# Self attention's front: products by position set between dense products and emptied by three engines, and layer norms batch by batch with idle products

## The chip, the cores and the metric

The kernel runs on one core of a Trainium2 chip. The metric is the device time of one execution in microseconds (us), median of several runs. TensorE is written PE in the profile (PEld is its weight load), VectorE is DVE, ScalarE is ACT, GpSimd is POOL, SyncE is SP. A line such as L612 is line 612 of the kernel before.

## The reference, cut to what matters

One layer of a Perceiver: cross attention over a long context, self attention with relative positions, and a feed-forward that is itself an attention with gated heads. Each of the three begins with a layer norm over the 512 features, and each adds to x. B is 4, T is 128, D is 512, with 16 heads of 32. The part that the change touches is the self attention and the layer norms ahead of it and behind it:

```python
def _layernorm(x, axis=-1, eps=1e-05):
    m = jnp.mean(x, axis=axis, keepdims=True)
    v = jnp.var(x, axis=axis, keepdims=True)
    return (x - m) / jnp.sqrt(v + eps)
...
    q, k, v = (proj(Wq), proj(Wk), proj(Wv))
    a_q = Eq[rel]
    a_k = Ek[rel]
    a_v = Ev[rel]
    content = jnp.einsum('bhld,bhmd->bhlm', q, k)
    rel_k = jnp.einsum('bhld,lmd->bhlm', q, a_k)
    rel_q = jnp.einsum('bhmd,lmd->bhlm', k, a_q)
    pos_pos = jnp.einsum('lmd,lmd->lm', a_q, a_k)
    scale = 1.0 / hd ** 0.5
    logits = (content + rel_k + rel_q + pos_pos) * scale
    attn = jax.nn.softmax(logits, axis=-1)
    out = jnp.einsum('bhlm,bhmd->bhld', attn, v) + jnp.einsum('bhlm,lmd->bhld', attn, a_v)
...
x = x + xattn(_layernorm(x), ctx, ctx, ...)
x = x + attn(_layernorm(x), ...)
x = x + ffn(_layernorm(x), ...)
```

All is in float32. rel is the distance of two positions, cut to plus or minus 64.

## The kernel before

The kernel has three stages: cross attention (to about 650 us), self attention (to about 790 us) and the feed-forward. Inside a stage every engine works through its instructions in the order in which the program writes them (`manual_schedule`), and waits only where data or a buffer is not ready. So the order of the lines is the order of each engine's queue.

**The layer norm.** `layernorm_T` (L145) takes the rows of four batches from four banks of PSUM. For the second and third norm (L562 and L844) it takes its `else` branch. DVE computes statistics by batch (L157, L158), ACT the root of the variance plus eps (L161), DVE its reciprocal (L190, L198) and minus mean over deviation (`nmr`, L191). Batches are taken in two pairs: one root and one reciprocal serve two batches. The first pair is normalised on ACT (L169), the second on DVE (L165). Then each batch is turned on PE with four transposes (L214) into one of two banks, and that bank is copied to `xT`, by ACT for batches 0 and 1 and by DVE for 2 and 3 (L215). Last, ACT copies the four rows of x out of PSUM (L207).

**Projections.** `project_T` (L217) and `project` (L224) are four dense 128x512 products each; the trace has two instructions for each product. q is projected into the two pairs of banks of `banks("q")` (L649), in the order ps[2], ps[3], ps[0], ps[1], and drained with a scale (L652), by DVE for c even and ACT for c odd. k goes into three single banks and one more (`bank`, `bank_z`), drained at L657. `values(b)` projects v for one batch, drained by ACT (L646).

**Products by position.** `spread` (L593) copies q or k into `z`, laid out by position, in 16 copies (L598), of which 6 are on ACT and 10 on DVE. For each position there is then one product of a 32-row table slice with a 32x64 block of z. `by_position` (L605) does eight positions for each of four row groups: 32 products, 64 instructions of the trace, filling four banks. `relative_k(n)` (L623) does this for q into the two pairs of banks of `ps4`, and ACT copies the four banks to `rk` (L627). `relative_q(n)` (L629) does it for k into three single banks and `bank_z`, and DVE adds the table `pos` while it writes `lg` (L634).

**Logits.** `logits(c)` (L683) turns `rk` back with 16 transposes into the two pairs of `ps4` (L687) and adds 32 content products (L700). `join` (L713) adds `lg` on DVE (L716), `largest` finds the maxima (L722), and ACT takes exponentials (L727).

[...] In the self attention they are three for `bank`, one for `bank_z` and two pairs for `banks`. All of them were the cross attention's before. The first product of q waits for DVE's and ACT's last copies of the layer norm, the four copies of x (L207) among them; the later products of q don't wait for those again.

## Time and profile before

| what | value |
|---|---|
| median of 3 runs | 875.72 us (874.93 to 877.7) |
| the profiled execution's own time | 875.97 us |
| its span, first to last instruction | 874.1 us |
| mean granted TensorE clock | 0.980 |
| PE busy | 830.6 us (95%) |
| DVE busy | 628.2 us (72%) |
| ACT busy | 436.5 us (50%) |
| POOL busy | 430.6 us (49%) |

Busy time in stretches of 25 us around the change, in us, with the granted clock:

| stretch | PE | DVE | ACT | POOL | clock |
|---|---|---|---|---|---|
| 625 to 650 | 22.27 | 16.64 | 0.00 | 0.36 | 1.00 |
| 650 to 675 | 19.80 | 7.99 | 5.54 | 0.00 | 0.86 |
| 675 to 700 | 25.00 | 13.24 | 15.71 | 0.00 | 1.00 |
| 700 to 725 | 23.27 | 8.31 | 10.59 | 0.00 | 0.93 |
| 725 to 750 | 17.22 | 17.81 | 16.48 | 8.16 | 0.87 |
| 750 to 775 | 21.36 | 12.43 | 17.87 | 8.16 | 0.86 |
| 775 to 800 | 17.78 | 16.77 | 10.11 | 7.32 | 0.80 |

An engine counts as busy while an instruction of its own runs; register, branch and semaphore instructions and the issue of transfers don't count. Matmuls overlap in the pipeline, so a busy PE is not a PE at its best. The granted clock is the share of full speed at which TensorE was let run. Where an engine is idle, the profile names the instruction whose end released it.

### The profile page before, as it was taken

Reading aid. Unit: us, or ns where it says so; the run is one execution under the profiler, and the core shown is the slowest. Engines: PE = TensorE matmul, PEld = TensorE weight load, DVE = VectorE, ACT = ScalarE, POOL = GpSimd, SP = SyncE. Lnnn points to the kernel's source line nnn. Section 1 sums busy time; section 2 is a strip of 40 time slices with the busy share of each in tenths; the row PEclk is TensorE's granted clock in tenths of the full one; section 3 lists DMA queues with packets and bytes.
Section 4 is the critical chain, followed back from the end, with each engine's and each line's share of the span. In section 5 each row is a group of like instructions: output and inputs, shape, how many; then the busy total and the mean of one; then the engine's idle time right before and its main releaser. Section 6 shows DMA issues by size and latency. Waiting matters only on the chain. (4 is left out here: it accounts for less than half of the span.)

```text
span 874.1 us, 16373 instructions
## 1 busy us (share of the span) xinstructions
PE 830.6 (95%) x7061; PEld 447.9 (51%) x7061; DVE 628.2 (72%) x616; ACT 436.5 (50%) x721; POOL 430.6 (49%) x289
## 2 busy tenths in 40 slices
PE   9999999999999999999999999999898997779998
PEld 5454544554544545445445445544443466664564
DVE  2059788878888888888889888788861637556663
ACT  3357455564464554554554555644411736843671
POOL 1236666566656567575675665667500002512152
PEclk9999999999999999999999999999998998798999
DMA  8130010110101101010010101010100212001101
GB/s 300 50 124 2 1 49 1 49 49 1 50 1 49 49 2 49 1 49 13 37 49 1 49 1 49 1 36 15 49 28 21 96 50 98 1 2 51 49 1 49
DMA packets 10905, 35.53 MB, mean 41 GB/s; under 512 B 977, under 2 KB 1138, under 8 KB 8786
## 3 DMA queue, kind: packets, MB, share of 16 engines
q1 hardware_dynamic: 8402, 29.43, 9.7%
q10 hardware_dynamic: 1632, 3.15, 1.1%
q0 software_dynamic: 800, 1.93, 0.9%
q8 instruction: 55, 0.90, 0.4%
q14 instruction: 16, 0.13, 0.0%
HBM read 33.45 MB, written 1.05 MB: 39 GB/s over the span
## 5 line engine op out<-in xcount | busy, mean ns | idle before, releaser
L328 DVE TENSOR_TENSOR sg<-sg,stat 128x2048 f32<-128x2048 f32 x128 | 288.2, 2282 | 1.2
L337 ACT ACTIVATE sg<-sg 128x2048 f32<-128x2048 f32 x64 | 122.4, 1912 | 246.8 <-DVE sg L328 246.8
L227 PE MATMUL ps_v<-w_xattn_Wv,ct 128*128 128x512 f32 x512 | 231.5, 596 | 3.7 <-ACT v L274 3.7
L220 PE MATMUL ps_k<-ct,w_xattn_Wk 128*128 128x512 f32 x480 | 221.9, 605 | 0.8 <-ACT pos L142 0.8
L343 POOL TENSOR_TENSOR sm<-sm,sg 128x1024 f32<-128x1024 f32 x46 | 108.6, 2360 | 145.5 <-ACT sg L337 143.3
L307 DVE TENSOR_TENSOR mx<-mx,ps_s 128x1024 f32<-128x1024 f32 x96 | 117.2, 1221 | 78.1 <-ACT sg L298 65.9
L227 PEld LDWEIGHTS ps_v<-w_xattn_Wv,ct 128*128 128x128 f32 x512 | 95.8, 190 | 129.9 <-issue 113.5
L220 PEld LDWEIGHTS ps_k<-ct,w_xattn_Wk 128*128 128x128 f32 x480 | 86.2, 189 | 94.1 <-issue 86.1
L298 ACT COPY sg<-ps_s 128x1024 f32<-128x1024 f32 x128 | 124.2, 1020 | 7.2 <-DVE mx L305 3.5
L344 POOL TENSOR_TENSOR sm<-sm,sg 128x1024 f32<-128x1024 f32 x46 | 108.8, 2366 | 3.6
L275 POOL TENSOR_TENSOR v<-v,row_xattn_bv 128x512 f32<-128x512 f32 x64 | 81.6, 1276 | 40.0 <-ACT v L274 40.0
L734 POOL TENSOR_TENSOR lg<-lg,rs 128x512 f32<-128x512 f32 x16 | 16.3, 1041 | 120.9 <-issue 112.3
L285 PE MATMUL ps_s<-qT,kT 32*128 32x128 f32 x2048 | 75.7, 283 | 0.1
L372 PEld LDWEIGHTS pso<-sg,v 128*32 128x32 f32 x1920 | 48.8, 109 | 47.5 <-DVE mx L307 22.0
L285 PEld LDWEIGHTS ps_s<-qT,kT 32*128 32x128 f32 x2048 | 63.3, 186 | 18.0 <-issue 17.0
L372 PE MATMUL pso<-sg,v 128*32 128x128 f32 x1920 | 64.6, 276 | 3.7 <-DVE acc L385 2.1
L341 POOL TENSOR_TENSOR sm<-sg 128x1024 f32<-128x1024 f32 x16 | 37.9, 2366 | 45.3 <-ACT sg L337 45.2
L268 ACT ACTIVATE kT<-ps_k,bk 128x512 f32<-128x512 f32 x64 | 44.2, 694 | 10.4 <-PE ps_k L220 5.9
L274 ACT COPY v<-ps_v 128x512 f32<-128x512 f32 x64 | 36.4, 569 | 8.5 <-PE ps_v L227 8.4
L385 DVE TENSOR_TENSOR acc<-pso,acc 128x512 f32<-128x512 f32 x54 | 37.0, 684 | 3.9 <-PE pso L372 3.9
L305 DVE TENSOR_TENSOR mx<-sg,ps_s 128x1024 f32<-128x1024 f32 x16 | 19.5, 1220 | 27.3 <-ACT sg L298 27.3
L964 POOL TENSOR_TENSOR e<-e,rs 128x512 f32<-128x512 f32 x16 | 16.3, 1041 | 41.8 <-DVE rs L963 41.8
(208 smaller groups left out, 817.0 us busy)
## 6 DMA issues: line engine op xcount, KB each, us to landing
ct<-in_ctxT SPq DMA_DIRECT2D x15, 1024.0 KB, 4.9
ev_win<-in_tabv SPq DMA_DIRECT2D x1, 2048.0 KB, 7.1
w_xattn_Wk<-in_xattn_Wk ACTq DMA_DIRECT2D x4, 256.0 KB, 8.0
ct<-in_ctxT SPq DMA_DIRECT2D x4, 256.0 KB, 6.7
x<-in_x SPq DMA_DIRECT2D x4, 256.0 KB, 8.2
w_xattn_Wv<-in_xattn_Wv ACTq DMA_DIRECT2D x1, 1024.0 KB
w_xattn_Wq<-in_xattn_Wq SPq DMA_DIRECT2D x1, 1024.0 KB, 10.3
w_xattn_Wo<-in_xattn_Wo ACTq DMA_DIRECT2D x1, 1024.0 KB, 5.4
```

What stands on the lines that cost most here:

```text
L220: nc.tensor.matmul(ps, lhsT=w[:, k, c * P : (c + 1) * P], rhs=src[:, k, :], start=(k == 0), stop=(k == C - 1))
L227: nc.tensor.matmul(ps, lhsT=src[:, k, b * T : (b + 1) * T], rhs=w[:, k, :], start=(k == 0), stop=(k == C - 1))
L268: nc.scalar.activation(kT[n, c], ps, AF.Identity, bias=bk[:, c : c + 1])
L275: nc.gpsimd.tensor_tensor(v[n, b], v[n, b], bv_row, ALU.add)
L285: nc.tensor.matmul(ps[i][:, cols], lhsT=kT[n, c][rows, cols], rhs=qT[rows, c, cols], start=True, stop=True)
L298: nc.scalar.copy(sg[n, c][:, k * HALF : (k + 1) * HALF], pss[n, c][k])
L307: nc.vector.tensor_tensor(mxs[n], mxs[n], pss[n, c][k], ALU.max)
L328: nc.vector.tensor_tensor(g, g, stat[:, row, :].unsqueeze(1).to_broadcast([P, NH * B, T]), op)
L337: nc.scalar.activation(sg[n, c], sg[n, c], AF.Exp, scale=SCALE)
L343: eng.tensor_tensor(t, t, g[:, 0:HALF], ALU.add)
L344: eng.tensor_tensor(t, t, g[:, HALF:], ALU.add)
L372: nc.tensor.matmul(ps[i * HD : (i + 1) * HD, b * T : (b + 1) * T], lhsT=v[n, b][:, h * HD : (h + 1) * HD], rhs=sg[n, c][:, f * T : (f + 1) ...
```

## The change

In the layer norm's `else` branch the batches are no longer taken in pairs. Each batch has a root of its own right after its statistics. Batches 0 and 1 get their reciprocal, `nmr` and ACT normalisation after the root of the next batch; batches 2 and 3 are normalised on DVE after all statistics. The third turned batch is now copied by ACT, and only the fourth by DVE. A new function `idle` puts products of a zero tile (`warm`) with itself into a bank that nobody reads: six ahead of the first transposes, three between the second and the third, three behind the fourth. This holds for the norms at L562 and L844; the first norm of the kernel takes the other branch. `warm` is allocated earlier; the twelve products at the start of the kernel stay.

In the self attention, q is projected into the four single banks. The blocks by position are placed between projections: q0 to q3, k0 to k2, rk0, k3, rk1, v0, rk2, v1, rk3, half of v2, lg0, the other half, lg1, half of v3, lg2, the other half, lg3. The lg blocks now use the two pairs of `ps4`, as rk does. Their drains are split: banks 0 and 1 stay with DVE (with the addition of `pos`); banks 2 and 3 are copied by ACT and the addition is done in place by GpSimd, except in the last block, where DVE does all four. The spread of k is 3 copies on ACT and 13 on DVE; that of q is as before.

The diff:

```diff
--- before.py
+++ after.py
@@ -142,7 +142,13 @@
         nc.scalar.copy(pos, ps)
         yield
 
-    def layernorm_T(src, pool, n, before=None):
+    warm = const.tile([P, P], F32, tag="warm", name="warm")
+
+    def idle(ps, k):
+        for _ in range(k):
+            nc.tensor.matmul(ps, lhsT=warm, rhs=warm, start=True, stop=True)
+
+    def layernorm_T(src, pool, n, before=None, keep=None):
 
 
 
@@ -182,26 +188,37 @@
             for b in range(B):
                 turned(b)
         else:
-            first, second = slice(0, 2), slice(2, 4)
-            statistics(0)
-            statistics(1)
-            root(first)
-            statistics(2)
-            nc.vector.reciprocal(rstd[:, first], rstd[:, first])
-            nc.vector.scalar_tensor_tensor(
-                nmr[:, first], in0=mv[:, first, 0], scalar=-1.0, in1=rstd[:, first], op0=ALU.mult, op1=ALU.mult
-            )
-            normalised_act(0)
-            normalised_act(1)
-            statistics(3)
-            root(second)
-            nc.vector.reciprocal(rstd[:, second], rstd[:, second])
-            normalised(2)
-            normalised(3)
+            def inverse(b):
+                nc.vector.reciprocal(rstd[:, b : b + 1], rstd[:, b : b + 1])
+
+            def to_act(b):
+                inverse(b)
+                nc.vector.scalar_tensor_tensor(
+                    nmr[:, b : b + 1],
+                    in0=mv[:, b, 0:1],
+                    scalar=-1.0,
+                    in1=rstd[:, b : b + 1],
+                    op0=ALU.mult,
+                    op1=ALU.mult,
+                )
+                normalised_act(b)
+
+            for b in range(B):
+                statistics(b)
+                root(slice(b, b + 1))
+                if b == 1 or b == 2:
+                    to_act(b - 1)
+            for b in (2, 3):
+                inverse(b)
+                normalised(b)
+
+            keep(6)
             turned(0)
             turned(1)
-            turned(2, nc.vector.tensor_copy)
+            keep(3)
+            turned(2)
             turned(3, nc.vector.tensor_copy)
+            keep(3)
 
             for b in range(B):
                 nc.scalar.copy(x1[:, b, :], src[b])
@@ -385,11 +402,9 @@
                 nc.vector.tensor_tensor(acc[:, c, :], pso[n, c], acc[:, c, :], ALU.add)
 
 
-        warm = const.tile([P, P], F32, tag="warm", name="warm")
         nc.vector.memset(warm, 0.0)
         ps = ps_o.tile([P, B * T], F32, tag="pso", name="warm_ps")[:, 0:P]
-        for _ in range(12):
-            nc.tensor.matmul(ps, lhsT=warm, rhs=warm, start=True, stop=True)
+        idle(ps, 12)
 
         softplus()
         nc.scalar.activation(small.tile([P, 1], F32, tag="rt", name="rt0"), eps, AF.Sqrt)
@@ -559,7 +574,8 @@
         nc.scalar.activation(small.tile([P, 1], F32, tag="rt", name="rt"), eps, AF.Sqrt)
         project_out(3)
 
-        xT = layernorm_T(out_ps, ps_g, 1)
+        idle_ps = ps_o.tile([P, B * T], F32, tag="pso", name="idle_ps1")[:, 0:P]
+        xT = layernorm_T(out_ps, ps_g, 1, keep=lambda k: idle(idle_ps, k))
 
 
     awq = load_w("attn_Wq", nc.sync)
@@ -590,12 +606,12 @@
 
         z = big.tile([P, 2, NJ, NF], F32, tag="z", name="z")
 
-        def spread(src, n):
+        def spread(src, n, on_act):
             for g in range(NG4):
                 for i in range(NH):
                     from_ = src[i * HD : (i + 1) * HD].rearrange("p c (b g j) -> p g j c b", b=B, g=NG4)
                     to = z[g * HD : (g + 1) * HD, n].rearrange("p j (c i b) -> p i j c b", i=NH, b=B)
-                    (nc.scalar.copy if (g * NH + i) % 5 in (1, 3) else nc.vector.tensor_copy)(to[:, i], from_[:, g])
+                    (nc.scalar.copy if (g * NH + i) % 5 in on_act else nc.vector.tensor_copy)(to[:, i], from_[:, g])
 
 
         rk = big.tile([P, NF, T], F32, tag="rk", name="rk")
@@ -627,46 +643,60 @@
                 nc.scalar.copy(rk[:, :, positions(g, n)], ps[g].rearrange("p (j f) -> p f j", f=NF))
 
         def relative_q(n):
-            ps = [bank(f"lg{n}_{g}") for g in range(3)] + [bank_z(f"lg{n}_3")]
+
+
+            ps, _ = banks(f"lg{n}")
             by_position(tabq, 1, n * J8, ps)
             for g in range(NG4):
                 at = positions(g, n)
-                nc.vector.tensor_tensor(
-                    lg[:, :, at],
-                    ps[g].rearrange("p (j f) -> p f j", f=NF),
-                    pos[:, at].unsqueeze(1).to_broadcast([P, NF, J8]),
-                    ALU.add,
+                from_ = ps[g].rearrange("p (j f) -> p f j", f=NF)
+                pos_ = pos[:, at].unsqueeze(1).to_broadcast([P, NF, J8])
+                if g >= 2 and n + 1 < NJ // J8:
+                    nc.scalar.copy(lg[:, :, at], from_)
+                    nc.gpsimd.tensor_tensor(lg[:, :, at], lg[:, :, at], pos_, ALU.add)
+                else:
+                    nc.vector.tensor_tensor(lg[:, :, at], from_, pos_, ALU.add)
+
+        v = one.tile([P, B, D], F32, tag="v", name="v2")
+
+        def values(b, between=None):
+
+            ps = bank(f"v{b}")
+            for k in range(C):
+                if between and k == C // 2:
+                    between()
+                nc.tensor.matmul(
+                    ps, lhsT=xT[:, k, b * T : (b + 1) * T], rhs=awv[:, k, :], start=(k == 0), stop=(k == C - 1)
                 )
-
-        v = one.tile([P, B, D], F32, tag="v", name="v2")
-
-        def values(b):
-            ps = bank(f"v{b}")
-            project(ps, awv, xT, b)
             nc.scalar.copy(v[:, b, :], ps)
 
-
-        ps, _ = banks("q")
-        for c in range(C):
-            project_T(ps[c - 2], awq, xT, c)
-            (nc.scalar.mul if c % 2 else nc.vector.tensor_scalar_mul)(qT[:, c, :], ps[c - 2], SCALE)
-        spread(qT, 0)
-        for c in range(C):
+        def queries(c):
+            ps = bank(f"q{c}") if c < 3 else bank_z("q3")
+            project_T(ps, awq, xT, c)
+            (nc.scalar.mul if c % 2 else nc.vector.tensor_scalar_mul)(qT[:, c, :], ps, SCALE)
+
+        def keys(c):
             ps = bank(f"k{c}") if c < 3 else bank_z("k3")
             project_T(ps, awk, xT, c)
             (nc.scalar.copy if c % 2 else nc.vector.tensor_copy)(kT[:, c, :], ps)
-        spread(kT, 1)
+
+
+        for c in range(C):
+            queries(c)
+        spread(qT, 0, (1, 3))
+        for c in range(C - 1):
+            keys(c)
+        relative_k(0)
+        keys(C - 1)
+        relative_k(1)
+        spread(kT, 1, (1,))
         values(0)
+        relative_k(2)
         values(1)
-        relative_k(0)
-        relative_q(0)
-        values(2)
-        relative_k(1)
+        relative_k(3)
+        values(2, lambda: relative_q(0))
         relative_q(1)
-        values(3)
-        relative_k(2)
-        relative_q(2)
-        relative_k(3)
+        values(3, lambda: relative_q(2))
         relative_q(3)
         ev_win = big.tile([P, T, HD], F32, tag="z", name="ev_win")
         nc.sync.dma_start(
@@ -841,7 +871,8 @@
         for b in range(B):
             for c in range(C):
                 nc.tensor.transpose(out_ps[b][:, c * P : (c + 1) * P], oT[:, c, b, :], ident)
-        xT = layernorm_T(out_ps, ps1, 2)
+        idle_ps = bank_z("idle")[:, 0:P]
+        xT = layernorm_T(out_ps, ps1, 2, keep=lambda k: idle(idle_ps, k))
```

## The prediction

> **What bounds the kernel now.** I read the page first: TensorE is busy for 95% of a span of 874.1 us, so time is lost where it waits or runs at a low granted clock. The slices put both after 640 us. I then asked for busy time by stretches of a few microseconds from 640 us on, for the chain of waits there, and for the groups of instructions with their shapes. The chain from the layer norm to the first logits is TensorE almost throughout (start, length, what; us):

> ```profile
> 656.38 1.97 ACT x L207 x4
> 658.34 0.73 issue
> 659.08 5.82 PE s_q L220 x8
> ...
> 664.98 0.70 DVE qT L652
> ...
> 665.73 7.15 PE s_q L220 x16
> 672.90 0.70 DVE qT L652
> ...
> 673.64 3.70 PE s_q L220 x8
> 677.34 13.73 PE s_k L220 x32
> ...
> 701.71 0.69 DVE lg L634
> ...
> 702.44 3.70 PE s_v L227 x8
> ...
> 716.31 2.06 ACT rk L627 x4
> ...
> 721.33 2.82 PE s_lg L612 x48
> 724.15 3.60 PE s_l L687 x16
> ...
> 729.14 2.48 DVE lg L716 x4
> ```

> The reader is to see four losses, and that the first projection comes after ACT's copies of x. That projection (8 instructions) takes 5.82 us; 16 of them take 7.15 a little later. Twice a projection waits for DVE to empty the bank pair of the one before it (664.98, 672.90). The values wait for DVE in the same way (701.71, and again at 709.91). And from 721.33 to 729.14 products take about twice their time. The stretches say why (length, then busy us and instructions of PE, PEld, DVE, ACT, POOL, then granted clock):

> ```profile
> 653.10:656.50 3.40, 1.39 (x9) 0.95 (x10) 2.39 (x9) 2.82 (x6) 0.00 (x0) 1.00 0.81 283
> 656.00:660.00 4.00, 2.75 (x9) 1.84 (x10) 2.38 (x4) 2.33 (x5) 0.00 (x0) 0.57 0.18 71
> 714.70:718.10 3.40, 3.40 (x127) 3.40 (x120) 0.02 (x1) 2.05 (x5) 0.00 (x0) 1.00 0.63 205
> 718.10:721.50 3.40, 3.20 (x84) 2.80 (x85) 2.47 (x4) 1.49 (x4) 0.00 (x0) 0.99 0.29 108
> 724.00:728.00 4.00, 4.00 (x24) 3.59 (x24) 2.48 (x4) 0.00 (x0) 0.00 (x0) 0.50 0.68 262
> 728.20:731.61 3.41, 1.93 (x40) 1.57 (x33) 2.47 (x5) 0.00 (x0) 0.00 (x0) 1.00 0.65 269
> 789.70:793.10 3.40, 3.40 (x16) 2.64 (x14) 2.38 (x4) 2.78 (x7) 2.64 (x7) 0.50 0.84 214
> ```

> After 1.39 us of work in 3.4 (41%) the clock is halved, and after 84 products by position in 3.4 us as well; 127 of them kept it. Asked in stretches of 0.2 us, it falls at 656.5, 721.5, 745.3, 755.5 and 782.9 and returns at 663.3, 728.3, 748.7, 762.3 and 793.1: whole multiples of some 3.4 us. The rows that price the engines:

> ```profile
> L634 DVE TENSOR_TENSOR lg<-s_lg,pos 128x512 f32<-128x512 f32 x16 | 9.9, 684 | 18.9 <-PE s_lg L612 18.9
> L627 ACT COPY rk<-s_rk 128x512 f32<-128x512 f32 x16 | 8.2, 599 | 5.2 <-PE s_rk L612 5.2
> L598 ACT COPY z<-qT 32x512 f32<-32x512 f32 x6 | 6.4, 1066 | 0.1
> L598 DVE COPY z<-qT 32x512 f32<-32x512 f32 x10 | 5.9, 593 | 4.5 <-ACT qT L652 4.4
> ```

> [...] in 789.70:793.10 TensorE did nothing but transposes and the clock returned at its end; I go by the trace. [...]

> **The change, part by part.** One dense 128x512 projection is 8 instructions of the trace, 13.90/4 = 3.475 us at full clock (s_k). A block by position is 64 instructions, 1.9 us (697.94 to 701.71 holds two). One drain is 0.51 us on ACT (2.05 for 4) and 0.62 on DVE (2.48 for 4).

> *Layer norm of line 562.* Statistics start at 650.69 as before (0.88 each). Now the root follows each one (0.29 on ACT), so the reciprocal and nmr of batch 0 come at 652.4 to 652.7 and its ACT normalisation at 652.75 rather than 653.60. DVE then does statistics 2, pair 1, statistics 3 and two normalisations of 0.76: xn0 is there at 653.5, xn1 654.5, xn2 655.4, xn3 656.2. The idle products (12 instructions, then 6 and 6, 0.107 each: 428/4, by columns) fill 652.36 to 653.65 and the gaps between transposes and end before the data or with it. The last transposes end at 657.2 and DVE's copy at 657.95, 1.0 earlier than the 658.98 of before. But the first q product waits, in both programs, for ACT's last x copy too (L207), since its banks come from the stage that ends there. ACT has one more copy ahead of those four: turned 2 at 656.55 to 657.15, then 2.06, to 659.2. So q starts at 659.3, before 659.08: +0.2; the earlier transposes are worth nothing. What counts is the clock: 653.1 to 656.5 goes from 41% busy to about 85%, and the next 3.4 us, with 1.5 of waiting, to 55%. In before, 57% kept the clock (1.93 of 3.41 us, 728.20 to 731.61). I take it as held: the first projection then takes 3.5 for 5.8.

> *Projections of q in four separate banks.* Both stalls (0.84, 0.78) go. From 659.3, four take 13.9: q ends at 673.2, where before it ended at 677.2: -4.0, made of +0.2 and -4.2 from clock and stalls. The q spread keeps its split and runs 673.9 to 680.4 beside k0 to k2 (10.4 us, to 683.6): hidden; if it were later than that, rk0 would wait.

> *Blocks between dense products.* From 673.2: k0 k1 k2 683.6; rk0 685.5; k3 689.0; rk1 690.9; v0 694.4; rk2 696.3; v1 699.8; rk3 701.7; half v2 703.5. lg0 now shares the four banks with rk and waits for rk3's ACT copies (to 703.85): 0.4 lost. lg0 705.8, half v2 707.6, lg1 709.5, half v3 711.2, lg2 713.1, half v3 714.85, lg3 716.75. Here each drain (two ACT, two DVE) needs 1.3 us and has the 1.75 of a half projection: hidden, with 0.4 to spare; if not, each block loses 0.5 or so. The k spread is now 13 on DVE, 13 x 0.593 = 7.7, from kT at 689.8 to 697.7, and 3 on ACT behind rk1's copies (693.0 to 696.2); lg0 needs it at 703.9. From k0 to lg3's end: 43.55 us; before 724.15 - 677.18 = 46.97. The difference, -3.4, is the two stalls (1.5) and half clock on lg3 (2.0).

> *GpSimd additions.* Six. The trace has no such addition here; near rows are 1.04 (L734) and 1.27 (L839). I take 1.3, bounds 1.0 and 2.6. They end at 716.8; the join needs them at 721.6. At 2.6 they would be 1 us late.

> *Tail.* The new wait: logits(0) uses the bank pairs of lg3, so its transposes wait for two of the four DVE drains, 716.8 to 718.1, with all of PE's queue behind them. Then 1.13 + 1.13 + a gap of 0.1 + 1.17: join at 721.6. Before, lg3's end to join took 4.99 at half clock; now 4.85. -0.1.

> Sum: -4.0 - 3.4 - 0.1 = -7.5 at the join (729.14). From there to the output transposes (784.36) the instructions are unchanged; half-clock stretches there (745.3 to 748.7, 755.5 to 762.3) cost perhaps 2.6 us, and a new phase may move them: 0, bounds -2.6 and +1.5.

> *Last layer norm (line 844).* TensorE is cold here after 5.1 us without work (782.9), so 12 idle instructions cost up to 12 x 0.213 = 2.6 us, from 788.0, while xn0 would be ready at 788.3 and starts at 789.27 now. With the window's end at 789.7, they end at 790.15 and the rest runs at full clock: q at 793.9, as now (793.97). A window ending at 787.8 gives -0.9, at 791.2 +0.8. I take 0. Weight loads move by a few us, earlier or later, and all have over 20 us of slack.

> Own time of the profiled execution: 875.97 (1.87 around the span). 875.97 - 7.5 = 868.5; the median of before, 875.72, lies 0.25 under it. I forecast 868.5.

> **Rivals.**
> - *Half clock in the tail.* lg3, counted at the weight that 88 products by position seem to have (below the limit, though 94% busy), and the 1.35 us wait make a window like 653.10:656.50. Logits(0) would then take 2 to 3 us more and logits(1) perhaps 1: 872. For it: those two rows. Against: the half projection in front must fall outside the window, about 3 phases in 10.
> - *The clock still drops in the first norm*, because 55% is too little in that phase, or because products of zeros don't count: half rate for two windows from about 660, +3.4: 872. Against: 24 of the zero products open the kernel in 4.6 us and the next 32 dense instructions take 13.99, full clock; and the 57% above.
> - *Downstream phase turns favourable*, and the cold stretches shrink: 866. Nothing in the profile decides it.
> - *Slower: single blocks pull the clock down in the front.* If one block of 1.9 us in a window is too much, each drop is two windows, 6.8 us at half rate, 3.4 us lost. Three such drops (10.2) exceed 7.5 and decide it; five give 885.5. Against: two blocks in a row and a stall (697.9 to 702.4) kept 1.00.

> **How the numbers follow.** Forecast 0.53, tail 0.22, norm 0.12, phase 0.08, slower 0.05. Low end 865.2 (downstream -2.6 and -0.9, rounded up), high 873.0 (either drop, and 0.8 in the last norm). About 0.3%, 2.6 us, is what a measurement can tell: faster 0.88, within 0.07 (both drops, or one with all else against), slower 0.05.

> **What would show it.** Right: clock 1.00 from 650 to 717; s_q in one piece of 13.9 that starts after the x copies; no wait for lg within the values; join near 721.6. Wrong: a drop of the clock between 660 and 715, the k spread or GpSimd named as what lg0 or the join waited for, or TensorE without work for over 2 us before logits(0).

## The result, and the profile after

The changed kernel takes 871.75 us (median of 5 runs, 869.01 to 874.15) beside 875.72 of the kernel before (5 runs, 874.93 to 877.7): 0.9945 of it, with a 95% interval of 0.9922 to 0.9969. That is 4.0 us faster; the forecast was 868.5, so 3.25 us of the promised gain are missing. The profiled execution took 871.75, its span 869.8, at a mean clock of 0.986.

To see where they went, both traces are cut at the same four places: the first statistics of the second layer norm, the join of logits(0), the start of the output transposes, and the first projection behind the last norm.

| stretch of the profiled execution (us) | before | after | difference | forecast |
|---|---|---|---|---|
| span's start to the second norm's first statistics | 650.69 | 653.22 | +2.53 | 0 |
| from there to the join | 78.45 | 71.88 | -6.57 | -7.5 |
| join to the start of the output transposes | 55.22 | 56.02 | +0.80 | 0 |
| from there to the last norm's q | 9.61 | 8.60 | -1.01 | 0 |
| the rest | 80.13 | 80.08 | -0.05 | 0 |
| sum (span) | 874.1 | 869.8 | -4.3 | -7.5 |

So most of the gain in the changed stage arrived; the rest was lost in places where the forecast charged nothing. The chain of waits of the changed kernel (start, length, what; us):

```profile
634.30 4.54 PE ps_out L544 x6
...
653.22 0.71 DVE st L163
...
659.50 1.97 ACT x L224 x4
...
661.50 14.00 PE s_q L237 x32
675.50 10.30 PE s_k L237 x24
685.80 1.94 PE s_rk L628 x64
687.75 3.63 PE s_k L237 x8
...
706.38 2.23 PE s_lg L628 x64
708.61 1.91 PE s_v L668 x4
...
718.24 1.96 PE s_lg L628 x64
...
720.22 1.30 DVE lg L658 x2
721.52 0.14 issue
721.65 1.06 PE s_l L717 x8
...
725.10 2.48 DVE lg L746 x4
727.59 0.60 DVE nm L752
728.23 0.03 issue
728.26 1.28 ACT L757
729.55 5.50 ACT lg L757 x28
```

q is one piece of 14.0 us behind the x copies, with no stall. From there to 720.20 TensorE follows TensorE without a wait, dense product, block, dense product, and the block at 718.24 takes 1.96 where lg3 took twice its time before. (The piece at 706.38 holds a wait of some 0.3 us inside the block, for ACT's copies of rk3.) The new wait of the tail is there: the transposes at 721.65 wait for two DVE drains (720.22). And there is a piece that the chain of before didn't have: 1.28 us of ACT at 728.26, for which the trace names no tile.

The clock's falls at 604.1, 634.8, 740.6, 754.3 and 778.2 fit one grid of 3.413 us, within 0.1 us; I lay the windows on that grid (length, then busy us and instructions of PE, PEld, DVE, ACT, POOL, then clock):

```profile
600.67:604.08 3.41, 1.34 (x44) 1.15 (x48) 3.04 (x3) 3.07 (x3) 1.60 (x2) 1.00 0.00 0
...
631.39:634.80 3.41, 1.58 (x33) 1.11 (x34) 2.21 (x3) 0.00 (x0) 0.00 (x0) 1.00 0.00 0
634.80:638.22 3.42, 3.42 (x5) 1.35 (x4) 1.64 (x1) 0.00 (x0) 0.00 (x0) 0.50 0.00 0
...
655.28:658.69 3.41, 3.00 (x27) 2.71 (x25) 3.23 (x10) 3.01 (x6) 0.00 (x0) 1.00 0.68 240
658.69:662.11 3.42, 2.08 (x14) 1.50 (x13) 0.88 (x2) 2.54 (x5) 0.00 (x0) 1.00 0.17 67
...
720.13:723.55 3.42, 1.82 (x19) 1.59 (x16) 2.48 (x4) 0.00 (x0) 0.00 (x0) 1.00 1.05 387
```

The two windows of the norm are 88% and 61% busy and keep the clock, as forecast with 85% and 55%. The tail's window, 53%, keeps it too. But long before the change's place, windows with 1.34 us of work (39%) and 1.58 (46%) bring half-clock stretches at 604.08 and 634.80. The trace of before has the same work there, and its own grid (through its falls at 656.55 and 721.41) cuts it elsewhere:

```profile
629.25:632.66 3.41, 1.99 (x68) 1.45 (x56) 2.27 (x1) 0.00 (x0) 0.00 (x0) 1.00 0.02 5
632.66:636.07 3.41, 2.61 (x6) 1.06 (x6) 2.88 (x2) 0.00 (x0) 0.00 (x0) 1.00 0.00 0
```

1.99 and 2.61 us in neighbouring windows keep the clock. In the chains the stage is 0.84 us late by 626 us (ps_sum at 626.25, before 625.41), and the six products of ps_out at 634.30 take 4.54 where they took 2.84: 0.84 + 1.70 make the 2.53 us. The 0.84 doesn't come from the fall at 604.08: the same instructions are as late ahead of it (VectorE's sum at 602.18 stands at 603.03). It comes from the opening of the kernel, TensorE before and after:

```profile
1.06 4.62 PE L392 MATMUL warm_ps<-warm 128*128 128x128 f32 x24 [1.06 <-DVE warm L389]
5.52 13.99 PE L400 MATMUL ps_k<-ct,w_xattn_Wk 128*128 128x512 f32 x32
...
1.06 5.49 PE L149 MATMUL warm_ps<-warm 128*128 128x128 f32 x24 [1.06 <-DVE warm L405]
6.34 14.10 PE L415 MATMUL ps_k<-ct,w_xattn_Wk 128*128 128x512 f32 x32
```

The twelve zero products that open both kernels take 5.49 us instead of 4.62, and the projection behind them ends 0.93 later. The grid, carried back, has a boundary at 4.6 us in the trace of before and at 6.75 in this one. Whether the change sets the grid or the phase of an execution does is asked below.

### The profile page after: what moved, and what is told of

Its sections match the earlier page's. It is cut to its first block, busy times and chain, and to the rows that moved or that the text cites. A ratio compares the mean times of both kernels' runs of the same rounds, so it can differ in the third digit from the quotient of the medians.

```text
span 869.8 us, 16501 instructions
## 1 busy us (share of the span) xinstructions
PE 831.1 (96%) x7109; PEld 450.1 (52%) x7109; DVE 625.6 (72%) x617; ACT 438.8 (50%) x730; POOL 437.9 (50%) x295
## 3 DMA queue, kind: packets, MB, share of 16 engines
q0 software_dynamic: 800, 1.93, 0.9%
## 5 line engine op out<-in xcount | busy, mean ns | idle before, releaser
L656 POOL TENSOR_TENSOR lg<-lg,pos 128x512 f32<-128x512 f32 x6 | 7.4, 1263 | 85.9 <-ACT lg L655 85.9
## 6 DMA issues: line engine op xcount, KB each, us to landing
w_xattn_Wq<-in_xattn_Wq SPq DMA_DIRECT2D x1, 1024.0 KB, 10.4
```

## The experiments

My theory after this: the missing time is the table load on the chain (1.3 us) and the late start ahead of the change (2.5 us), which comes from the grid's phase, not from the edit; within the stage, the norm's work holds the clock and the separate banks and the order do the rest. The rivals: the load is late in any case and costs nothing; the edit itself delays the earlier stage; the batch order of the norm, not the idle products, holds the clock; one half of the change brings the whole gain.

**The table load.** ACT_TABLE_LOAD takes 1.28 us at each of its eight places in both traces. The first stands ahead of the kernel's first exponential, each other one ahead of the first instruction with another function than the last among exponential, logarithm and root; here it is the exponential's. The timeline of ACT, before (start, length, engine, line, operation):

```profile
722.35 1.28 ACT L727 ACT_TABLE_LOAD   x1
732.25 0.40 ACT L727 ACTIVATE lg<-lg,nm 128x128 f32<-128x128 f32 x1 [8.62 <-DVE nm L722]
```

and after:

```profile
728.26 1.28 ACT L757 ACT_TABLE_LOAD   x1 [9.39 <-DVE nm L752]
729.55 0.40 ACT L757 ACTIVATE lg<-lg,nm 128x128 f32<-128x128 f32 x1
```

Before, the load ran behind ACT's last rk copies, and only the exponential waited for the maxima (nm). After, the load itself waits for them: 9.39 us of ACT doing nothing, and then 1.28 on the chain. The input of the exponential now has further writers, ACT and GpSimd beside DVE. At five of the other places the load stands ahead of a call on one column (the tiles named rt, 0.20 us each), which the kernel has early; here it has none. The experiment gives ACT an exponential of one column early:

```diff
         relative_q(3)
+        nc.scalar.activation(small.tile([P, 1], F32, tag="rt", name="rt_exp"), eps, AF.Exp)
```

> The changed kernel with one small exponential on ScalarE (one element a row) put behind the last block by position, so that the exponential's table is loaded ahead of the wait for the maxima. Theory 'table load exposed': the 1.28 us load leaves the chain; from the join to the output transposes 56.0 us becomes 54.7, and the whole is 1.3 us under the changed kernel, near 870.4. Rival 'only the phase of the clock moved': the load is hidden anyway by VectorE's maxima, that stretch stays at 55.5 to 56.5 and the whole at 871 to 872.

Measured: 866.73 (866.57 to 869.37), 0.9899 [0.9872, 0.9926] of before. ACT's timeline:

```profile
716.33 1.28 ACT L701 ACT_TABLE_LOAD   x1
717.62 0.20 ACT L701 ACTIVATE rt_exp<-eps 128x1 f32<-128x1 f32 x1
725.74 0.40 ACT L758 ACTIVATE lg<-lg,nm 128x128 f32<-128x128 f32 x1 [7.91 <-DVE nm L753]
```

Join to first exponential: 3.17 us, for 4.45 after and 3.11 before. Join to output transposes is 53.63, where 54.7 was expected, and the median 866.73 lies below the expected 870.4: its norm starts at 650.68, since no window of the earlier stage lost the clock, so a good part of these 5 us is phase. A repeat beside other runs:

> The preload kernel once more. Theory 'table load exposed': from the first join to the first exponential 3.1 to 3.2 us, as before the change (3.11), where the changed kernel has 4.45; median 1 to 3 us under the changed kernel's 871.7, that is 869 to 870.7. Rival 'its first four runs were lucky in their phase and the load is worth nothing': 871 to 872.

Measured: 869.39 (866.85 to 873.23), 0.9911 [0.989, 0.9932]; its profiled execution fell into an unlucky phase (statistics at 652.66, a half-clock stretch from 722.5), and the 3.17 stayed. Over ten runs the preload stands at some 869.1, the changed kernel over eleven at 871.74. The 1.28 us are settled: the long form (4.44 or 4.45) is in every trace with the new lg drains and no preload, five of them; the short one (3.11 to 3.17) in all others, nine. Why the load waits is argued and not shown. The change of projections and drains brings it (the front alone has it, the norm alone doesn't), and the further writer is the part of it that touches the exponential's input; but no run gives lg back to one writer with all else kept.

**Each half alone.** The projections and blocks of the change on the norm of before, and the norm alone with the order of before:

```diff
-            for b in range(B):
-                statistics(b)
...
-            keep(6)
+            first, second = slice(0, 2), slice(2, 4)
+            statistics(0)
+            statistics(1)
+            root(first)
...
```

> The changed kernel's projections and blocks by position, with the layer norm of before (pairs, no idle products). Theory 'two gains that add': the clock falls after the norm as in before, so the first projection takes 5.8 us again and the last norm 9.6; from the first statistics to the join about 74.5 us (before 78.45, changed 71.9), the whole 2.5 to 4 us above the changed kernel. Rival 'the gain lies in the order of the projections alone': the whole within 1 us of the changed kernel.

> Before with the new layer norm and the idle products only. Theory 'two gains that add': the first projection takes 3.5 us, the stalls of q and v and the half clock at the logits stay; statistics to join about 76 us, last norm 8.6 to 9.6, the whole 2 to 3.5 us under before, near 873. Rival 'norm is worth nothing': within 1 us of before.

Measured: front alone 875.82 (12 runs), 0.9994 [0.9982, 1.0005]; norm alone 876.35 (12 runs), 0.9998 [0.998, 1.0017]. Neither can be told from before, though together they give 0.9945; 873 was expected of the norm alone, and the front alone is 4.1 above the changed kernel, just over the 2.5 to 4 expected. In the stage each brings a part: first statistics to join 75.54 and 76.89, for 78.45 before and 71.88 with both, so 2.9 and 1.6 of the 6.6; both traces lose the clock in the tail (the front alone at 721.9; in the norm alone the 16 transposes behind lg3 take 3.67 us, the next 16 2.26). q takes 16.12 and 16.00, for 18.10 and 13.84. The two stalls are worth 2.0 and the clock 2.1, together 4.1 of the 4.26. The norm alone, in its chain:

```profile
660.48 3.71 PE s_q L237 x8
...
664.28 0.70 DVE qT L669
...
665.02 7.15 PE s_q L237 x16
...
672.20 0.70 DVE qT L669
...
672.94 3.70 PE s_q L237 x8
```

Full clock (3.71 for 5.82), both stalls still there. That the 2.9 and 1.6 us aren't in the spans (874.0 and 874.1, for 874.1) has causes outside this stage that the two traces show. The front alone takes 57.87 from the join to the output transposes, for 55.22: 1.34 of that is the table load (4.45 for 3.11), the rest goes with more half clock there (13.7 us for 10.2). The norm alone starts its statistics at 652.20, 1.5 late, with a fall of the clock at 633.2. Each is one trace, for medians of 12 runs.

**Without the idle products.** The batch order stays.

```diff
-            keep(6)
             turned(0)
             turned(1)
-            keep(3)
             turned(2)
             turned(3, nc.vector.tensor_copy)
-            keep(3)
```

> The changed kernel without its idle products, all else kept. Theory 'the idle products hold the clock': TensorE is then busy for under half of the window after the cross attention, the clock falls near the first projection, which takes 5.5 to 6 us (or one of the next two does), and the last norm has its q 0.5 to 1 us later; the whole 2 to 4 us above the changed kernel. Rival 'the quicker norm is enough': the first four projections stay at 14.0 us and the whole within 1 us of the changed kernel.

Measured: 874.39 (20 runs), 0.9968 [0.9953, 0.9982]. The windows on its grid that end where the clock falls:

```profile
654.60:658.01 3.41, 1.62 (x11) 1.18 (x12) 3.22 (x11) 3.29 (x7) 0.00 (x0) 1.00 0.62 199
...
719.45:722.86 3.41, 2.19 (x65) 1.88 (x64) 1.19 (x2) 0.58 (x1) 1.57 (x2) 1.00 0.55 152
```

1.62 us (47%) in the norm, and the clock is gone at 658.01; q takes 15.65. So the products of zeros hold it, and the batch order doesn't. That this isn't the luck of one phase is shown by all traces together: the five without idle products (three of before, the front alone, this one) lose the clock behind a norm window of 1.31 to 1.77 us, and the nine with them, in either order, keep it, with 2.08 or more.

**Idle products on the norm of before** (two pairs), the reverse of that:

```diff
+            keep(6)
             turned(0)
             turned(1)
-            turned(2, nc.vector.tensor_copy)
+            keep(3)
+            turned(2, nc.vector.tensor_copy)
             turned(3, nc.vector.tensor_copy)
+            keep(3)
```

> The changed kernel with the norm's old order (pairs, two copies on each engine), idle products kept. Theory 'the idle products count, the batch order does not': q still starts 8.3 to 8.5 us after the first statistics and takes 14 us, last norm within 0.3 us of 8.6; statistics to join 71.8 to 72.3. Rival 'batch order matters': q starts 0.5 to 1 us later or runs at half clock in part, statistics to join over 73.

Measured: 871.06 (870.43 to 871.92), 0.9939 [0.9926, 0.9952], not to be told from the changed kernel beside it. q takes 13.81, and starts 7.90 us after the first statistics, where 8.3 to 8.5 was expected. That is 0.49 before the 8.39 of the kernel before: there q waited for VectorE's last turned batch (done at 658.98; the x copies were done at 658.33), and at full clock the last eight transposes take 1.35 us for 1.83. And it is 0.38 before the 8.28 of the changed kernel, where the x copies end last (661.45): with the extra ACT copy ahead of them they end 8.23 after the first statistics, here 7.64. So in this norm the batch order costs 0.38. In the last norm it pays. There the time from the output transposes to q goes with when the clock returns: in the kernel before 9.61 us where it returned 8.7 us after the transposes began (793.1), and 9.08 where it returned 4.3 after (before_third). The traces in which it does so 3.8 to 4.3 us after compare fairly: 9.08 (pairs, before_third, without idle products) and 9.24 (pairs, with), 8.44 (batches, without) and 8.60 (batches, with). The batch order is worth 0.64 there and the idle products cost 0.16, so far as single traces tell, and what the batch order costs and brings in the two norms nearly cancels.

**The unchanged kernels again**, for the stage ahead of the change:

> The changed kernel once more, for its spread. Theory 'phase decides what is left of the gain': the times span 4 to 6 us, and the trace has the first statistics of the second norm anywhere from 650.7 to 653.2 us, with a half-clock stretch in the cross attention's last 50 us whenever it is late, while statistics to join stays within 0.3 us of 71.9. Rival 'the change slows the cross attention': the statistics start at 653 us again.

> The kernel before, for the place of its half-clock stretches. Theory 'phase, not the change, makes the second norm late': in this trace or the next one a stretch of half clock lies between 600 and 640 us and the statistics start after 651.5 us; statistics to join stays within 0.3 us of 78.45. Rival 'the change slows the cross attention': 650.7 in both.

> The kernel before a third time; as the run ahead of it: with phase as the cause, at least one of the two has its statistics after 651.5 us; with the change as the cause, both start at 650.7.

Measured: the changed kernel 871.74 (869.49 to 874.02), 0.9949 [0.9934, 0.9965]; the kernel before 876.6 and 877.9 in one run each. The norm's first statistics come at 652.69 in the changed kernel's second trace, and at 650.75 and 652.91 in those of before. The third trace of before has the half-clock stretches of the changed kernel at the same work (603.4 to 606.8, 634.1 to 637.6). Compared instruction by instruction with the first trace of before, the late start is made of the same two parts in both programs (us):

| trace | grid boundary in the opening | late at 600 | added by a fall at 633 to 635 | first statistics |
|---|---|---|---|---|
| before | 4.61 | 0 | none | 650.69 |
| before, second | 4.76 | 0.07 | none | 650.75 |
| before, third | 6.09 | 0.53 | 1.70 | 652.91 |
| changed | 6.75 | 0.84 | 1.70 | 653.22 |
| changed, second | 5.69 | 0.40 | 1.63 | 652.69 |
| changed with preload | 4.65 | 0.02 | none | 650.68 |

In all fourteen traces the late start is this sum, to 0.04 us (the one with zero products in this stage, below, adds 0.5 for them). The fall at 633 to 635 is in eight of them and adds 1.50 to 1.70; the fall at 603 to 604, in six, adds nothing. So the late start belongs to the phase of an execution. The edit isn't needed for it; that it makes a late phase more frequent, so few traces can't exclude. The second trace of the changed kernel also shows the tail rival (windows on its grid):

```profile
719.07:722.48 3.41, 1.81 (x34) 1.50 (x27) 2.48 (x4) 0.00 (x0) 0.00 (x0) 1.00 0.96 359
722.48:725.90 3.42, 3.42 (x40) 3.02 (x39) 0.00 (x0) 0.00 (x0) 0.00 (x0) 0.50 1.03 424
```

k0 to join takes 51.37 then, for 49.76. Of the nine traces with the new order and nothing to hold the tail, five have it (this one, e1_again, the front alone, no idle products, and e7_held below, whose products sit elsewhere).

**A shorter norm and even drains.** The x copies of batches 0 and 3 move ahead, the last one to DVE, so that q waits for two; and the drains of each bank pair are split one to ACT and GpSimd, one to DVE, so that the tail waits for one DVE drain. With the preload:

```diff
+            nc.scalar.copy(x1[:, 0, :], src[0])
             turned(2)
+            nc.vector.tensor_copy(x1[:, 3, :], src[3])
             turned(3, nc.vector.tensor_copy)
...
-            for b in range(B):
+            for b in (1, 2):
                 nc.scalar.copy(x1[:, b, :], src[b])
...
-                if g >= 2 and n + 1 < NJ // J8:
+                if g % 2:
```

> The preload kernel with two more edits: ScalarE and GpSimd take banks 1 and 3 of every lg block (the last one too), and the copies of x in the norm are spread (one on ScalarE ahead of the third turned copy, one on VectorE, two behind). Theory 'q waits for the x copies, the logits for two drains on one engine': q starts 7.5 us after the first statistics, not 8.3, and TensorE waits 0.7 us before the logits, not 1.47; statistics to join 70.4. Rival 'something else is next': no change of either, 71.9.

Measured: 868.64 (868.35 to 869.6), 0.9912 [0.99, 0.9925]. Its chain:

```profile
657.80 0.99 ACT x L225 x2
...
658.83 14.00 PE s_q L238 x32
...
715.71 1.96 PE s_lg L629 x64
...
717.68 0.70 DVE lg L659
...
718.41 0.59 ACT lg L656
...
719.05 1.97 PE s_l L719 x16
721.01 1.17 PE s_l L732 x32
```

q starts 7.30 us after the statistics, 0.98 earlier, near what was expected. The tail didn't follow: the wait is 1.40 for 1.47, where 0.7 was expected, since the two drains of a pair, on DVE and on ACT, don't run beside each other: ACT's copy (718.41) waits for DVE's drain of the same pair of banks, in lg2 (713.69, then 714.41) as in lg3. In the changed kernel, where ACT has a pair to itself, the two engines started within 0.06 us (lg2: 716.36 and 716.42). The transposes then run in one piece, and the stretch k0 to join is 49.54; statistics to join is 70.67, for 70.4 expected. Its interval lies below that of the changed kernel beside it; with the preload alone, no difference is shown.

**Holding the clock in the earlier stage.** Eight zero products at each of the two places where windows run empty before the norm, on top of the last kernel:

```diff
+        idle(bank("idle_tail")[:, 0:P], 8)
         attend(*done)
...
+        for _ in range(8):
+            nc.tensor.matmul(out_ps[0][:, 0:P], lhsT=warm, rhs=warm, start=False, stop=False, skip_group_check=True)
         scaled(n, 0)
```

> The one before it (x copies and drains spread, table preloaded) with 16 more zero products in two waits of the cross attention's end: 8 ahead of the first attend after the loop, 8 (added to an output bank as zeros) ahead of the last scaled block. Theory 'late starts are half clock in those waits': the statistics start at 650.5 to 651.2 in every run, the times lie within 3 us of each other and the median is 1 to 2 us under the kernel without them. Rival 'the phase is set elsewhere': the spread stays 4 us or more.

Measured: 871.03 (868.26 to 871.33), 0.9926 [0.9911, 0.9941], 2.4 above the kernel without them, where 1 to 2 below was expected. The clock stays at 1.00 from 600 to 640, as meant, but the statistics come at 652.06, later than the 651.53 of the kernel without them, whose clock fell once (604.3). The chain shows why:

```profile
631.03 1.98 PE ps_out L556 x16
633.01 1.05 PE pso L390 x32
```

The 16 instructions of zeros stand on the chain: the products behind them start at 633.01, for 632.42, and the statistics 0.53 later. Both traces are 0.9 late at 600 us already, from the opening, which no hold here can mend. The first hold stands in a wait and costs nothing, but the fall that it prevents costs nothing either. The second costs 0.5, and the kernel without it had no fall there in this phase; where that fall comes it costs 1.5 to 1.7, so this hold may pay in other phases, which these runs don't show. And this trace's phase loses the tail: its window 717.09 to 720.51 holds 2.02 us of work in 49 instructions and the clock falls at its end, where in the kernel without the holds 2.02 us in 39 instructions kept it.

**Holding the tail.** Six zero products (12 instructions) ahead of logits(0), with the preload:

```diff
+        idle(bank_z("idle_l")[:, 0:P], 6)
         ps = logits(0)
```

> The preload kernel with six zero products between the last block by position and the logits, where TensorE waits 1.47 us for VectorE's drains. Theory 'the wait before the logits decides whether the clock falls there': no half clock between 715 and 730 us, statistics to join 71.8 to 72.1 in the trace, and the median 0.3 to 1 us under the preload kernel run beside it. Rival 'the blocks by position themselves are too little': the clock still falls near 721 in the trace or the median is the same.

Measured: 869.65 (866.47 to 873.03), 0.992 [0.9896, 0.9945], beside 869.39 with the preload alone: no gain shown. The trace has them in the wait (TensorE's timeline):

```profile
720.40 1.60 PE L149 MATMUL s_idle_l<-warm 128*128 128x128 f32 x12
721.93 2.26 PE L718 MATMUL s_l<-ident,rk 128*128 128x128 f32 x16
```

Its clock stays, and k0 to join takes 49.77; but so it does in the changed kernel's first trace without them. A fall in the tail costs 1.2 to 1.6 us (k0 to join 50.98 to 51.37 in the five traces that have it, for 49.5 to 49.8 in the four that haven't), some 0.8 on average: too little to show in the spread of these medians. Whether the hold helps at all is open.

## Why the prediction held, and where 3.25 us went

*The direction and the main term were right.* Clock and stalls of q: forecast -4.2, measured 18.10 to 13.84, -4.26, of which the halves show 4.1. The windows of the norm held with the busy shares named. The x copies set q's start (659.50, then 661.50). No wait for lg stands within the values, and the k spread and the drains are hidden. VectorE's drains take 0.685 us beside GpSimd's additions, 0.684 before: no cost of that pairing shows. GpSimd's addition was taken at 1.3 and costs 1.26, an idle product at 0.107 and costs 0.112 (0.67/6); GpSimd did no work on these additions after 719.55, with the join at 725.10.

*Start of q:* forecast +0.2 after the first statistics, measured -0.11 (8.39 to 8.28). The term was small and its sign wrong. In the kernel before, q followed VectorE's last turned batch (658.98) and not the x copies, which were done at 658.33. Two more slips carry nothing: the low end, 868.5 less 2.6 and 0.9, is 865.0 and not 865.2, and the "24 zero products" of the opening are twelve, of two instructions each.

*Blocks between dense products: the mis-sized term.* From the start of k0 to the end of lg3 I summed 43.55; it is 44.84. The sum used full dense runs (3.475, halves 1.75) and blocks of 1.9. A dense product with a block on either side takes 3.63 (three: +0.4), a half 1.91 (four: +0.6), and a block 1.94 (+0.3). Spread over the fifteen changes of kind, the 1.3 us are about 0.1 each. lg0's wait for rk3's copies was near what was told (0.3 for 0.4).

*Tail:* the wait was given 1.35, by sums of drains; it is 1.47, and lg3's end to the join is 4.90 for 4.85.

*The step that was missed: "From there to the output transposes (784.36) the instructions are unchanged".* They are, but what they wait for isn't. The table load moved from behind the rk copies (722.35, hidden) to behind the maxima (728.26): +1.34 from join to first exponential, 1.28 of it the load. My guess at the reason, which no run shows, is the further writer that the addition on GpSimd gives to the exponential's input. Behind the first exponential 0.54 is gained, which makes the +0.80 of the table; the same instructions take 50.46 to 52.43 there in the three traces of before, so that is within what the phase does.

*The phase ahead of the change.* "Statistics start at 650.69 as before" took one execution for the kernel. The fourteen traces lie between 650.68 and 653.50, those of before between 650.69 and 652.91. The range had no term for it. In this pair of profiled executions, 2.53 of the 3.2 us that the spans miss are this; how much of it stands in the medians is open.

*Last norm:* forecast 0 with -0.9 as the low bound, measured -1.01; 0.64 is the batch order, which I hadn't counted there, less 0.16 for the idle products; the rest, some 0.5, I put down to the clock.

That the time came as near as it did is in part luck: this gain and the 0.54 behind the exponential, 1.55 together, were in no term of the sum and came in its favour (without them 871.75 would be 873.3, above the range), against a load and a late start that were in no term either.

The rivals: half clock in the tail occurs, in five of nine traces, for 1.2 to 1.6 us and not 3 to 4; my three phases in ten were too few. Single blocks never pulled the clock down: between the norm and the tail no trace of the new order falls. Zero products do count (in the norm's window 1.62 us without them lost the clock, 2.08 with them kept it), which ends the rival that they don't.

## What to carry to other kernels

When the drains of a tile move to other engines, look where the table load of its readers on ACT stands: here, with ACT and GpSimd as further writers of lg, it stood behind the wait for the maxima, 1.28 us, in all five traces without the preload (that the writers are the reason isn't shown), and one early use of the function, 0.20 us on an idle ACT, put it back. Where a window holds about half of its length in work (at 633 us 47% lost the clock and 49% kept it), the windows have to be laid on their grid: two executions cut the same work differently, and the start of a stage moves by 2.2 us in the unchanged kernel. Before a half-clock stretch is blamed for a delay, the same instructions are compared ahead of it and behind it: here one such stretch cost 1.7 us and the other nothing. Idle products paid where the engine would have waited anyway and dense products came next (q in 13.84 us, for 15.65 without them); on the path they cost time, 0.5 us in the one place.
